# Industry's products as one stream of steps: two tiles ahead of layer 1's loop, 14 steps in each iteration

## Chip, cores and metric

The kernel runs on one core of one Trainium2 chip. The metric is the device time of one execution in microseconds. TensorE is called PE, VectorE DVE, ScalarE ACT, GpSimd POOL, and SyncE, which issues most transfers, SP.

## The reference

Four graph layers follow one another, each with a residual and a layer norm: `x = layernorm(x + layer(x))`. There are B = 8 batches, N = 2048 nodes and 64 features; `adj` is 2048 x 2048 and sparse. The change lies in layer 1, of which this matters:

```
h = x @ W
... agg, beta: attention of 64 hyperedges over the nodes
all_he = elu(beta * h + (1 - beta) * agg)
g = sum over a node's hyperedges e of coefs1[e] * all_he[e]
industry = (adj / deg) @ (x @ W_ind)
pair = stack([industry, g])
coefs2 = softmax(tanh(pair @ fcW + fcb) @ av)
out = sum over the pair of coefs2 * pair
```

So for each node there are two vectors, `industry` and `g`, and a two-way softmax mixes them.

## The kernel before

The nodes are split into NT = 16 tiles of 128. A row of a tile holds all 8 batches x 64 features, 512 numbers. The matrix of zeros and ones behind `adj` (the mask) is written to DRAM once in layer 0, one 1 MB block for each tile, and later layers load it again (`mask_tile`, and `mask_parts` for a block in four pieces).

A product of the mask with a 512-wide operand is split into a high and a low part of the operand, so one tile of Industry is 16 steps (`mt` = 0 to 15, one for each tile of the summed index) of two 128x512 matmuls, in `times_mask` (L1418). They add up in one PSUM buffer called `acc`, which comes from a pool with a single buffer. After the 16th step ACT reads it, multiplies it by the node's scale and writes it to SBUF as `ind` (L766), and DVE reads it again for the difference `dlt = industry - g` (L770).

Layer 1's main loop has NT + 3 iterations and is a software pipeline. At iteration t, different tiles are at different stages:

- `units` (marks u, v and s, for tiles t+1, t+2 and t): the hyperedge part, which ends in g. `sx`, `ST`, `gates`, `tau` and `ch0` prepare a tile; `gp0 z0 exp0 e0 w0` and `gp1 z1 exp1 e1 w1` are its two halves, each a chain PE, DVE, ACT, DVE, POOL; the two halves of all tiles share one PSUM buffer `gp`, so the next `gp` waits for the `e` before it. `dp` and `t3` belong to the fourth membership, and `ga`, `red` and `g` add up.
- `industry` (marks p and q): the 16 steps in pairs, and then `ind` and `dlt`.
- `mix_and_norm` (marks m, o and f, for tiles t-1, t-2 and t-3): `tr0 sT0 fc0 th0` for g, `tr1 sT1 fc1 th1` for industry, then `sub df sw`, and then the mix, the sum with the residual and the layer norm (`mult r s centre sq var rstd x2`).

The order within an iteration is written out by hand in the string `turns`, one word for each stage, and `program_order` fixes it on PE, DVE, ACT and POOL. SP's order is not fixed by it. A mark `p.i` is one pair of steps, four matmuls. In `turns` of the kernel before there are eight of them, and the last two stand at the end of the iteration.

Tile 0's product is done before the loop. `industry_early` makes a function `go_on(n)` that issues n more steps of it, and calls of it stand in the gaps of the end of layer 0 (5 and 3 steps) and of the start of layer 1 (4, 1, 2 and the rest, which is one), where the hyperedge attention is worked out in a chain of short instructions (`trhe`, `fche`, `sep`, `dnp`). Between them and the loop stand the stages of tile 0's unit and the first ones of tile 1's, and there are no steps of Industry there, nor in iteration t=0.

Tiles of SBUF that live for a short time are placed by hand in 16 homes (`b0_0` to `b0_15`), listed for each kind in `homes`.

Of the kernel before, what the change touches and what calls it, by code (L numbers as in the profile page):

```python
# [8 lines left out]
F32 = mybir.dt.float32  # L9

F32R = mybir.dt.float32r
AF = mybir.ActivationFunctionType
# [45 lines left out]
def r_(ap):  # L58
    return ap.bitcast(F32R)
# [3 lines left out]
def kernel(  # L63
# [450 lines left out]
    def layer1(  # L514
# [21 lines left out]
        with tc.tile_pool(name="fa", bufs=2) as fa:  # L536
# [10 lines left out]
            with program_order():  # L547
# [10 lines left out]
                    nc.vector.tensor_tensor(r_(dst[low]), full[low], dst[low], ALU.subtract)  # L558

                nc.vector.scalar_tensor_tensor(he, he, 1.0, agg, op0=ALU.min, op1=ALU.max)  # L560
                early[0](4)
                tr = ps_tr.tile([P, NP, P], F32, tag="tr", name="trhe")
                for pr in range(NP):
                    transpose(tr[:, pr, :], he[:, pr * P:(pr + 1) * P])
                heT = fa.tile([P, NP * P], F32, tag="hs", name="heT", bufs=3)
                nc.scalar.copy(heT, tr.rearrange("p r c -> p (r c)"))
                parts(agg1, agg)
                early[0](1)
                fc = ps_mm.tile([P, 2, QW], F32, tag="mm", name="fche")
                for h in range(2):  # L570
                    rs = slice(h * 64, (h + 1) * 64)
# [4 lines left out]
                    b_view(he), b_view(agg), -1.0,  # L576
                    vecs[:, 2, :].unsqueeze(1).to_broadcast([P, B, C]), op0=ALU.add, op1=ALU.mult,
                )
                early[0](2)
                sp = ps_tr.tile([P, QW], F32, tag="sm", name="sep")  # L580
                for b in range(B):
                    nc.tensor.matmul(
# [11 lines left out]
                nc.vector.tensor_copy(sums[:, 1, :], ese)  # L594
                parts(ext, sums)

                early[0](NT)
                dn = ps_tr.tile([P, NT, 2, B], F32, tag="tr", name="dnp")
                for j in range(NT):
                    nc.tensor.matmul(  # L600
# [15 lines left out]
        fw = stack.enter_context(tc.tile_pool(name="fw", bufs=2))  # L616
        mjp = stack.enter_context(tc.tile_pool(name="mj1", bufs=2))
        turn = {}
        homes = {"g": (0, 1, 2, 3), "dlt": (4, 5, 7), "ind": (14,), "r": (8, 9, 10),
                 "xr": (6, 12), "sq": (13,)}  # L620

        def row(tag, name):
            turn[tag] = turn.get(tag, -1) + 1
            home = homes[tag][turn[tag] % len(homes[tag])]
            return own.tile([P, BC], F32, tag=f"b0_{home}", name=name)
# [123 lines left out]
            dst[j] = g  # L749
            yield "g"  # L750

        def industry(j):

            if j:
                a = mask_tile(mjp, j, "l1")
                acc = ps_acc.tile([P, BC], F32, tag="acc", name=f"ind_{j}")
            else:
                acc = early[1]
            for mt in range(NT):
                if j:  # L760
                    times_mask(acc, a, i_hi, i_lo, mt)
                if mt % 2 == 1:
                    yield "i"
            sdeg = cols_of["sdeg"][:, j:j + 1]
            ind = row("ind", f"ind_{j}")
            nc.scalar.activation(ind, acc, AF.Copy, scale=sdeg)  # L766
            ind_of[j] = ind
            yield "ind"
            dlt = row("dlt", f"dlt_{j}")
            nc.vector.scalar_tensor_tensor(  # L770
                dlt, acc, sdeg, g_of[j], op0=ALU.mult, op1=ALU.subtract
            )
            dlt_of[j] = dlt
            yield "dlt"

        def mix_and_norm(j):

            ind, g, dlt = ind_of[j], g_of[j], dlt_of[j]
            xr = row("xr", f"xr_{j}")
            nc.sync.dma_start(xr, kept[j])
            r = row("r", f"r1_{j}")
# [75 lines left out]
        def layer2(j):  # L860
# [24 lines left out]

        g_of, ind_of, dlt_of = {}, {}, {}
        unit = {j: units(j, g_of) for j in range(NT)}
        mixer = {j: mix_and_norm(j) for j in range(NT)}  # L890
        product = {j: industry(j) for j in range(NT)}
        first = "sx ST gates tau ch0"
        second = "gp0 z0 exp0 ch1 dp t3 e0 w0 gp1 z1 exp1 e1 w1"
        turns = (
            "q.ind u.gp0 u.z0 q.dlt m.xg m.tr0 v.sx m.sT0 v.ST u.exp0 u.ch1 m.fc0 m.tr1 u.dp "
            "o.mult m.sT1 p.i m.th0 f.rstd u.t3 u.e0 p.i o.r m.fc1 v.gates u.w0 o.s u.gp1 p.i "
            "v.tau p.i m.th1 u.z1 s.ga p.i v.ch0 u.exp1 m.sub u.e1 o.centre s.red u.w1 f.x2 p.i "
            "m.df s.g o.sq m.sw o.var p.i p.i"
        )

        done = set()
# [18 lines left out]
        last = layer2_steps()  # L920
        with program_order():
            run(unit, 0, first)
            run(unit, 0, second)
            run(unit, 1, first)
            for t in range(NT + 3):
                now = {"p": (product, t), "q": (product, t - 1), "u": (unit, t + 1), "v": (unit, t + 2),
                       "s": (unit, t), "m": (mixer, t - 1), "o": (mixer, t - 2),
                       "f": (mixer, t - 3)}
                for turn_ in turns.split():
                    who, what = turn_.split(".")  # L930
                    run(*now[who], what)
                    if t > NT and 0 <= now[who][1] < NT:
                        next(last, None)
            a_first = mask_parts(own, 0, (11, 15, 0, 1), "l2")
            for _ in last:
                pass
            for j in range(NT):
                nc.gpsimd.tensor_tensor(
                    b_view(x2[:, j, :]), b_view(x2[:, j, :]),
                    bias2_sb.unsqueeze(1).to_broadcast([P, B, C]), ALU.add,  # L940
                )
# [12 lines left out]
    def layer0(  # L954
# [3 lines left out]

        h_sb, wb, wa, vecs, av_sb, pm, es, hgr, aggp, rden, early = layer1s
        raws, msk, terms, resid, norm, srow = {}, {}, {}, {}, {}, {}
        x1s, xTs, hps, hss, mds = {}, {}, {}, {}, {}

# [275 lines left out]
                    denp[0], mds[j], es[:, j, :], start=j == 0, stop=j == NT - 1  # L1240
                )

        def industry_early():


            a = mask_parts(own, 0, (4, 6, 13, 14), "l1")
            acc = ps_acc.tile([P, BC], F32, tag="acc", name="ind_0")

            def steps():
                for mt in range(NT):  # L1250
                    for part in (y_hi, y_lo):
                        nc.tensor.matmul(
                            acc, r_(a[:, mt, :]), r_(part[:, mt, :]),
                            start=mt == 0 and part is y_hi, stop=mt == NT - 1 and part is y_lo,
                        )
                    yield

            going = steps()

            def go_on(n):  # L1260
                for _ in range(n):
                    next(going, None)

            return go_on, go_on, acc

        mhalf = tile("mhalf", "mhalf0", (P, B), 1)
        nc.vector.memset(mhalf, -0.5)
        denp = []
# [17 lines left out]
        with program_order():  # L1286
# [6 lines left out]
            for j in range(NT + 1):  # L1293
# [4 lines left out]
                for g in range(8):  # L1298
# [9 lines left out]
                    elif g == 1:  # L1308
                        when(j - 1, normed, 1)
                        if j == NT:  # L1310
                            denp.append(
                                ps_p.tile([P, 2, 2, 4 * C], F32, tag="pp", name="denp")[:, 0, 0, 0:B]
                            )
                            denominators(0, NT - 1)
                            early.extend(industry_early())
                            early.pop(0)(5)
                        if first:
                            degrees(0)
                        when(j + 1, scaled, 0)
                    elif g == 2:  # L1320
                        when(j - 1, normed, 2)
                        when(j + 1, first_terms)
                    elif g == 3:
                        when(j - 2, project)
                        if j + 1 < NT:
                            for _ in product(j + 1):
                                pass
                        when(j - 1, to_features)
                        when(j + 1, compare, 0)
                        when(j + 1, scaled, 1)  # L1330
                        if j == NT - 2:
                            for t in range(len(kept_i)):
                                for y, kept_part in zip((y_hi, y_lo), kept_i[t]):
                                    nc.sync.dma_start(y[:, t, :], kept_part)
                        when(j + 2, mask, 0)
                        when(j + 2, mask, 1)
                    elif g == 5:
                        when(j + 1, compare, 1)
                        if j:
                            next(flags, None)  # L1340
                    elif g == 6:
                        when(j + 1, second_term)
                        when(j - 1, scores)
                        if j < NT:
                            when(j - 2, gather)
                        else:
                            project(NT - 1, h_first=True)
                            denominators(NT - 1, NT)
                            gather(NT - 2)
                            nc.vector.tensor_scalar(rden, denp[0], TINY, None, op0=ALU.max)  # L1350
                            nc.vector.reciprocal(rden, rden)
                    elif g == 7:
                        when(j + 1, degrees)
            early[0](3)
            gather(NT - 1)


    def short_program(top):
# [57 lines left out]
        def times_mask(acc, a, hi, lo, mt):  # L1416
            for part in (hi, lo):
# [2 lines left out]
                    start=mt == 0 and part is hi, stop=mt == NT - 1 and part is lo,  # L1420
                )

        def ln_tiles(pool):
            return lambda shape, tag, name: pool.tile(shape, F32, tag=tag, name=name)

# [4 lines left out]
        with tc.tile_pool(name="l0", bufs=1) as l0, tc.tile_pool(  # L1430
# [15 lines left out]
            with tc.tile_pool(name="l0s", bufs=2) as l0s, tc.tile_pool(  # L1446
# [2 lines left out]
            ) as ps_p:  # L1449
                layer0(  # L1450
                    own, l0s, rawp, mskp, ps_acc, ps_tr, ps_p, w_sb, emb_sb, bias_sb, bad, deg,
                    y_hi, y_lo, (h_sb, wb, wa, vecs, av_sb, pm, es, hgr, aggp, rden, early),
                )
                s1, dinv = cols_of["s1"], cols_of["dinv"]
                nc.vector.tensor_tensor(deg, deg, s1, ALU.mult)
# [694 lines left out]
```

## Time and profile before

| what | value |
|---|---|
| median of 3 runs | 1318.43 us (1313.73 to 1319.35) |
| the profiled execution, its own time | 1318.67 us |
| its span, first to last instruction | 1316.8 us |
| instructions | 19976 |
| granted PE clock, mean of the span | 0.973 |
| layer 1's loop, t=1 to t=15 (first gp to the last ind) | 760.7 to 1004.5 us |
| one steady iteration | 16.15 us |

The page gives, for each engine, the time it was busy. The chain of waits follows the work that ended last back from the last instruction, and its shares say which engine the end was waiting for. A table by stretch of time gives each engine's busy time and number of instructions in it, then the clock that PE was granted (1.00 is full speed), the share of the DMA engines that was busy, and GB/s. In a timeline, a bracket at the end of a line gives the time that the engine was idle before the instruction, and what ended it.

### The profile page before, as it was taken

What the parts mean: (1) busy time and instruction counts of PE and PEld (TensorE: products, weight loads), DVE (VectorE), ACT (ScalarE), POOL (GpSimd) and SP (SyncE); (2) the same over time, 40 slices, a digit from 0 to 9 for tenths busy, and PEclk for the clock granted to TensorE, in tenths of its full rate; (3) what the DMA queues carried; (4) which work ended last, traced back from release to release, by engine and by line L of the source; (5) the groups of instructions that cost most, each with busy time, mean ns of one, the idle gap of its engine ahead of it and who ended that gap; (6) DMA issues with size and microseconds to landing.
All of it is one profiled execution on the core that took longest, in us unless ns stands there. A gap on an engine that the chain in (4) does not pass through costs nothing.

```text
span 1316.8 us, 19976 instructions
## 1 busy us (share of the span) xinstructions
PE 1259.5 (96%) x7708; PEld 1002.4 (76%) x7708; DVE 885.0 (67%) x1595; ACT 368.4 (28%) x837; POOL 483.5 (37%) x403
## 2 busy tenths in 40 slices
PE   7999799999999999999999699999998899999996
PEld 6777588888888888888887467777776788888885
DVE  5555268888777877888664568878874655565544
ACT  3000001221122222221222356666664621111111
POOL 1000264444444444444411468888873600000000
PEclk9999799999999999999998589999998999999998
DMA  9887733332333332222272212222220133234551
GB/s 294 238 222 136 215 100 101 107 98 100 107 107 107 106 102 94 94 94 102 81 240 67 103 71 98 96 96 97 81 96 0 50 144 115 109 128 147 176 185 70
DMA packets 100791, 157.22 MB, mean 119 GB/s; under 512 B 12880, under 2 KB 64464, under 8 KB 94672
## 3 DMA queue, kind: packets, MB, share of 16 engines
q1 hardware_dynamic: 98208, 151.65, 35.7%
q10 hardware_dynamic: 2304, 4.20, 0.8%
q8 instruction: 63, 1.03, 0.3%
q0 software_dynamic: 176, 0.02, 0.1%
q14 instruction: 40, 0.33, 0.1%
HBM read 118.08 MB, written 37.76 MB: 118 GB/s over the span
## 4 chain that ended last, share of the span: by engine, by line
PE 89%; DVE 3%; DMA 2%; issue 2%; ACT 2%; POOL 1%; SPq 0%; ACTq 0%; DVEq 0%; POOLq 0%
PE pp L1104 25%; PE a L1418 18%; PE y2p L1067 9%; PE ind L1418 9%; PE y1p L490 8%; PE fc L805 3%; PE df L814 2%; PE gp L705 1%; PE yp L1508 1%; PE try L165 1%; PE trm L165 1%; PE aggp L1224 1%; PE hp L1192 1%; PE sgp L1171 1%; PE red L746 1%
## 5 line engine op out<-in xcount | busy, mean ns | idle before, releaser
L1115 DVE SCALAR_TENSOR_TENSOR r<-pp,emb_sb,r 128x256 f32<-128x256 f32 x512 | 247.4, 483 | 114.8 <-PE pp L1104 100.6
L1104 PE MATMUL pp<-w_sb,xT 64*128 64x256 f32 x1024 | 160.4, 390 | 1.7 <-DVE r L1115 1.7
L1104 PE MATMUL pp<-w_sb,y1T 64*128 64x256 f32 x1024 | 153.5, 376 | 0.0
L1104 PE MATMUL pp<-w_sb,y2T 64*128 64x256 f32 x1024 | 153.5, 376 | 0.0
L1053 POOL TENSOR_TENSOR r<-xs,bn 128x256 f32<-128x256 f32 x32 | 22.7, 731 | 277.2 <-issue 245.4
L1104 PEld LDWEIGHTS pp<-w_sb,xT 64*128 64x128 f32 x1024 | 94.4, 186 | 25.1 <-issue 14.9
L490 PE MATMUL y1p<-x_hi,m 128*128 128x512 f32 x256 | 106.2, 415 | 6.9 <-ACT x_hi L436 6.9
L1104 PEld LDWEIGHTS pp<-w_sb,y1T 64*128 64x128 f32 x1024 | 99.7, 187 | 10.9
L1104 PEld LDWEIGHTS pp<-w_sb,y2T 64*128 64x128 f32 x1024 | 99.6, 187 | 11.0
L1067 PE MATMUL y2p<-y_hi,msk 128*128 128x512 f32 x256 | 103.5, 404 | 0.0
L490 PE MATMUL y1p<-x_lo,m 128*128 128x512 f32 x256 | 103.0, 402 | 0.0
L1418 PE MATMUL ind<-y_hi,mj_l 128*128 128x512 f32 x240 | 101.7, 424 | 0.0
L1067 PE MATMUL y2p<-y_lo,msk 128*128 128x512 f32 x256 | 101.5, 397 | 0.0
L1418 PE MATMUL a<-v_hi,mj_l 128*128 128x512 f32 x256 | 100.1, 392 | 0.0
L1418 PE MATMUL a<-v_lo,mj_l 128*128 128x512 f32 x256 | 99.9, 391 | 0.0
L1418 PE MATMUL a<-y_lo,mj_l 128*128 128x512 f32 x240 | 95.1, 396 | 0.0
L1418 PE MATMUL a<-y_hi,mj_l 128*128 128x512 f32 x240 | 94.9, 396 | 0.0
L1418 PE MATMUL ind<-y_lo,mj_l 128*128 128x512 f32 x240 | 94.6, 394 | 0.0
L1009 POOL TENSOR_TENSOR ms<-msk,srow 128x1024 f32<-128x1024 f32 x32 | 89.8, 2807 | 5.3 <-DVE ms L1022 5.3
L737 POOL TENSOR_TENSOR ez<-ez,coef 128x1024 f32<-128x1024 f32 x32 | 69.8, 2182 | 56.3 <-DVE ez L735 54.3
L1001 DVE TENSOR_SCALAR msk<-adj 128x1024 fp32r<-128x1024 f32 x32 | 63.7, 2024 | 9.2 <-DMA adj<-in_at 9.2
L490 PEld LDWEIGHTS y1p<-x_hi,m 128*128 128x128 f32 x256 | 49.6, 194 | 19.0 <-ACT x_hi L436 6.9
(279 smaller groups left out, 2391.8 us busy)
## 6 DMA issues: line engine op xcount, KB each, us to landing
mj_l<-mask SPq DMA_DIRECT2D x46, 1024.0 KB, 4.9
raw<-in_at SPq DMA_DIRECT2D x32, 512.0 KB, 5.1
adj<-in_at SPq DMA_DIRECT2D x64, 256.0 KB, 3.8
mask<-msk SPq DMA_DIRECT2D x32, 512.0 KB, 4.6
xraw<-in_xn SPq DMA_DIRECT2D x8, 512.0 KB, 4.6
oh<-oh SPq DMA_DIRECT2D x32, 128.0 KB, 2.8
xT<-in_xt SPq DMA_DIRECT2D x16, 256.0 KB, 3.0
xs<-in_xn SPq DMA_DIRECT2D x16, 256.0 KB, 2.9
```

What stands on the lines that cost most here:

```text
L165: nc.tensor.matmul(dst, src, ident, start=True, stop=True, is_transpose=True)
L490: nc.tensor.matmul(accs[q][jj], r_(m[:, t, jj * P:(jj + 1) * P]), r_(part[:, mt, :]), start=i + h + t == 0 and part is x_hi, stop=i == 3 a ...
L737: nc.gpsimd.tensor_tensor(by_b(ez), by_b(ez), per_b(coef, 2 * i, 2), ALU.mult)
L805: nc.tensor.matmul(fc[:, h, :], fcw_sb[rs], sT[rs], start=True, stop=True)
L814: nc.tensor.matmul(df[:, b:b + 1], th[:, b % 2, (b // 2) * P:(b // 2 + 1) * P], av_sb, start=True, stop=True,)
L1001: nc.vector.tensor_scalar(r_(m), raws[j][h], 0.0, None, op0=ALU.is_gt)
L1009: nc.gpsimd.tensor_tensor(ms, m, srow[j].unsqueeze(1).to_broadcast([P, 8, P]), ALU.mult)
L1053: nc.gpsimd.tensor_tensor(r[:, 4 * bq * C:4 * (bq + 1) * C] .rearrange("p (h l c) -> p h l c", h=2, l=2), swapped(terms[j]["xs"], bq), bn. ...
L1067: nc.tensor.matmul(acc, r_(msk[j, mt // 8][:, mt % 8, :]), r_(part[:, mt, :]), start=mt == 0 and part is y_hi, stop=mt == NT - 1 and part ...
L1104: nc.tensor.matmul(pp[:, h, pl, :], terms[j][name][rs, 2 * bq + pl], w_sb[rs, k, dq * 4 * C:(dq + 1) * 4 * C], start=k == 0, stop=k == K - 1,)
L1115: nc.vector.scalar_tensor_tensor(rb, ppv[:, :, dd, :], emb_sb[:, j, d:d + 1], rb, op0=ALU.mult, op1=ALU.add)
L1418: nc.tensor.matmul(acc, r_(a[:, mt, :]), r_(part[:, mt, :]), start=mt == 0 and part is hi, stop=mt == NT - 1 and part is lo,)
```

## The change

The products of all tiles become one stream of 256 steps, held by an object `products` of a new class `industry`; `go_on(n)` issues the next n steps, whatever tile they belong to. When a tile's 16th step is issued, ACT's read of the accumulator is issued right behind it, and the result `ind` is kept in SBUF, in one of three homes (14, 11 and 15 in turn), until the mixing takes it. The masks of tiles 0 and 1 are loaded in four pieces each.

Ahead of the loop the stream now goes on by 5, 3, 4, 1, 2 and 3 steps where it did before (3 in place of the one that was left), then by 8 between tile 0's `t3` and `e0`, and by 6 after tile 1's `sx` to `ch0`, which now stand ahead of tile 0's `z1`. That is 32 steps, two tiles. In the loop each iteration has seven `p.i`, 14 steps, so that t=0 to t=15 issue the other 224. `dlt` moves to the mixing and is computed from `ind` in SBUF. The order in `turns` is new as a whole.

```diff
-        homes = {"g": (0, 1, 2, 3), "dlt": (4, 5, 7), "ind": (14,), "r": (8, 9, 10),
+        homes = {"g": (0, 1, 2, 3), "dlt": (4, 5, 7), "r": (8, 9, 10),
...
-                early[0](NT)
+                products.go_on(3)
                 dn = ps_tr.tile([P, NT, 2, B], F32, tag="tr", name="dnp")
...
-            sdeg = cols_of["sdeg"][:, j:j + 1]
-            ind = row("ind", f"ind_{j}")
-            nc.scalar.activation(ind, acc, AF.Copy, scale=sdeg)
-            ind_of[j] = ind
-            yield "ind"
-            dlt = row("dlt", f"dlt_{j}")
-            nc.vector.scalar_tensor_tensor(
-                dlt, acc, sdeg, g_of[j], op0=ALU.mult, op1=ALU.subtract
-            )
...
+        products.mask_of = lambda j: mask_tile(mjp, j, "l1")
+        ind_of = products.sums
+
+        def mix_and_norm(j):
+            ind, g, dlt = ind_of[j], g_of[j], row("dlt", f"dlt_{j}")
+            nc.vector.scalar_tensor_tensor(dlt, ind, 1.0, g, op0=ALU.mult, op1=ALU.subtract)
             yield "dlt"
...
         turns = (
-            "q.ind u.gp0 u.z0 q.dlt m.xg m.tr0 v.sx m.sT0 v.ST u.exp0 u.ch1 m.fc0 m.tr1 u.dp "
-            "o.mult m.sT1 p.i m.th0 f.rstd u.t3 u.e0 p.i o.r m.fc1 v.gates u.w0 o.s u.gp1 p.i "
-            "v.tau p.i m.th1 u.z1 s.ga p.i v.ch0 u.exp1 m.sub u.e1 o.centre s.red u.w1 f.x2 p.i "
-            "m.df s.g o.sq m.sw o.var p.i p.i"
+            "u.gp0 p.i m.dlt m.xg p.i f.rstd m.tr0 v.sx s.ga m.sT0 u.z0 u.exp0 m.fc0 o.mult m.tr1 "
+            "v.ST v.gates m.sT1 u.ch1 p.i o.r m.th0 u.dp u.t3 u.e0 u.w0 s.red o.s u.gp1 m.fc1 "
+            "m.th1 p.i s.g u.z1 p.i p.i v.tau m.sub u.exp1 p.i o.centre o.sq u.e1 v.ch0 m.df f.x2 "
+            "m.sw u.w1 o.var"
         )
...
             run(unit, 0, first)
-            run(unit, 0, second)
+            run(unit, 0, "gp0 z0 exp0 ch1 dp t3")
+            products.go_on(8)
+            run(unit, 0, "e0 w0 gp1")
             run(unit, 1, first)
+            products.go_on(6)
+            run(unit, 0, "z1 exp1 e1 w1")
...
                     who, what = turn_.split(".")
+                    if who == "p":
+                        products.go_on(2)
+                        continue
...
+        class industry:
+            def __init__(self, own, ps_acc, hi, lo):
+                early_masks = [
+                    mask_parts(own, 0, (4, 6, 13, 14), "l1"), mask_parts(own, 1, (7, 8, 11, 12), "l1b")
+                ]
+                self.mask_of, self.sums = early_masks.__getitem__, {}
+                self.steps = self.rows(own, ps_acc, hi, lo)
+
+            def rows(self, own, ps_acc, hi, lo):
+                for j in range(NT):
+                    a = self.mask_of(j)
+                    acc = ps_acc.tile([P, BC], F32, tag="acc", name=f"ind_{j}")
+                    for mt in range(NT):
+                        times_mask(acc, a, hi, lo, mt)
+                        if mt == NT - 1:
+                            ind = own.tile(
+                                [P, BC], F32, tag=f"b0_{(14, 11, 15)[j % 3]}", name=f"ind_{j}"
+                            )
+                            nc.scalar.activation(
+                                ind, acc, AF.Copy, scale=cols_of["sdeg"][:, j:j + 1]
+                            )
+                            self.sums[j] = ind
+                        yield
+
+            def go_on(self, n):
+                for _ in range(n):
+                    next(self.steps, None)
```

## The prediction

> **What bounds the kernel now.** I read the page's busy shares first, then the chain of waits in order of time, then busy time by stretch, then the timeline at a tile's end.
>
> ```profile
> PE 1259.5 (96%) x7708; PEld 1002.4 (76%) x7708; DVE 885.0 (67%) x1595; ACT 368.4 (28%) x837; POOL 483.5 (37%) x403
> PE 89%; DVE 3%; DMA 2%; issue 2%; ACT 2%; POOL 1%; SPq 0%; ACTq 0%; DVEq 0%; POOLq 0%
> ```
>
> PE holds 89% of the chain, so what counts is PE's instructions and PE's waits. The chain inside one turn of layer 1's loop:
>
> ```profile
> 784.62 1.86 PE ind L1418 x8
> 786.48 1.06 PE fc L805 x4
> ...
> 788.19 2.75 PE ind L1418 x12
> 790.94 0.86 PE red L746 x2
> 791.80 0.93 PE ind L1418 x4
> ...
> 794.42 1.97 PE ind L1418 x8
> ```
>
> These 32 matmuls of Industry take 1.86 + 2.75 + 0.93 + 1.97 = 7.51 us, **0.235 us each**. The same place recurs every 16.15 us (788.19, 804.35, 820.50). By stretch (PE, PEld, DVE, ACT, POOL busy; granted clock; DMA):
>
> ```profile
> 733.20:741.30 8.10, 3.77 (x8) 2.04 (x9) 4.43 (x9) 3.34 (x13) 2.94 (x3) 0.71 0.68 259
> 747.20:754.70 7.50, 4.71 (x12) 2.83 (x12) 4.33 (x10) 3.33 (x13) 4.72 (x3) 0.50 0.00 0
> 754.70:760.70 6.00, 2.90 (x4) 1.19 (x5) 3.83 (x9) 2.58 (x7) 5.89 (x4) 0.50 0.12 44
> 764.10:780.00 15.90, 15.90 (x68) 10.84 (x68) 7.81 (x14) 7.47 (x18) 10.57 (x9) 0.90 0.10 35
> 796.39:812.54 16.15, 16.15 (x81) 11.60 (x81) 12.88 (x20) 11.13 (x29) 13.04 (x10) 1.00 0.27 98
> ```
>
> The last row is a steady iteration: PE is never idle, DVE has 3.3 us free, POOL 3.1, ACT 5. The first three are the lead-in: PE idles half the time (gaps of 4.34, 3.32, 2.79 and 3.07 us, each waiting for DVE's ez) and is granted half clock. There a 128x512 matmul takes a slot of 0.427 us (ind at 706.07, then 706.50), not 0.235. A tile's end:
>
> ```profile
> 795.99 0.40 PE L1418 MATMUL ind<-y_lo,mj_l 128*128 128x512 f32 x1
> 796.22 0.63 PE L705 MATMUL gp<-agg,oh 128*128 128x512 f32 x2
> 796.43 0.69 ACT L766 ACTIVATE ind<-ind,sdeg 128x512 f32<-128x512 f32 x1 [1.79 <-PE ind L1418]
> ```
>
> The tile's last matmul ends at 796.39 and ACT reads the accumulator until 797.12. Meanwhile PE goes on with gp, because the next tile's first matmul comes only at 800.61: today the read is covered.
>
> **What the skill says.** The Trainium skill, "TensorE: Matmul & The Clock Gate", Part 1, says that PE falls to half rate after an idle window of about 3.4 us and returns after a busy one, the windows running freely. The trace agrees: 0.427 against 0.235 us, and clock 0.50 over the gaps. The same page, "Architectural detail", says that matmuls stay in order and ACT and DVE are strict FIFO, so a wait holds up all behind it; the trace shows each engine in its written order. "PSUM — Partial Sum Buffer", the summary of rules, says to read one bank while the matmul runs in another. Industry has one accumulator (a pool of one buffer), and the kernel before shows only the covered case.
>
> **The change, part by part**, against the profiled run's own 1318.67 us (span 1316.8; the median of the runs is 1318.43, so the two may be used alike).
>
> *A. Fewer matmuls per iteration.* 28 in place of 32: 4 x 0.235 = 0.94 us less. I walked the new turns with the durations above. From gp0 at 0, PE does gp0, 8 ind (to 2.35), tr0, sx, fc0, tr1 (5.18), 4 ind, dp, red, gp1 (8.72), fc1 (9.78), 16 ind (13.54), df (15.22). What it waits for arrives in time: e0 on DVE ends near 6.4 (gp1 wants it at 8.07), sub near 12.3 (df at 13.54), e1 near 14.1 (the next gp0 at 15.22). POOL's 13.3 us fit. So 15.2 per iteration: for t = 2 to 15, 14 x 0.94 = **-13.1**.
>
> *B. Tile ends inside the iteration.* Two tiles are done ahead and a tile needs eight "p.i", an iteration has seven. So tile 2 ends at the first p.i of t=1, tile 3 at the second of t=2, on to the seventh of t=7; t=8 has none; then first to seventh again for t=9 to 15. On PE the new list puts nothing between p.i 1 and 2, nor between 4, 5, 6 and 7 (m.dlt, m.xg, s.g, u.z1, v.tau, m.sub, u.exp1 belong to other engines). An end at 1, 4, 5 or 6 thus exposes ACT's read, with all of PE's queue behind the next tile's first matmul. Price: 0.17 (the last matmul lasts 0.40, its slot is 0.23) + 0.04 + 0.69 + about 0.07 to start, + 0.09 because the first matmul after a break takes a slot of 0.32 (778.12 to 778.44): **1.05 us**, more than the iteration's gain. In t>=2 they are t = 4, 5, 6, 9, 12, 13, 14: 7 x 1.05 = 7.4. Bounds: 0 if something I overlooked covers them (a wait added to a queue without idle time gains nothing), 1.3 if ACT is behind with th1; I take 1.05. Besides, an end at 6 puts the read ahead of tau and exp1 on ACT, so e1 ends about 0.35 after PE wants it (twice), and an end at 2 makes sT0, and fc0 behind it, 0.25 late (twice): 1.2. Together **+8.6**.
>
> *C. The lead-in*, from sep (PE free at 726.71) to the start of t=2 (gp0 at 780.23).
> - go_on(3) ahead of dnp: before, one step stood there (1.06 us). Now that step ends tile 0, ACT reads it (+0.9), and four matmuls of tile 1 follow (4 x 0.427 = 1.7): dnp, and with it rec, hgr, sx, gp0, starts about 2.5 late (1.85 at full clock).
> - go_on(8): 16 matmuls after dp, which now ends near 739.4. Half clock at first, then full: about 4.5 us, of which 4.34 was idle. gp1 comes at about 744.3 instead of 741.33.
> - unit 1's sx and go_on(6): 12 matmuls, then ACT's read of tile 1 ahead of exp1 in ACT's queue, and unit 1's gates ahead of z1 on DVE. gp1 to the next gp0: 0.65 + 0.73 + 2.82 + 0.2 + 0.69 + 1.1 + 1.25 + 0.14 = 7.6 against 5.9. So t=0 starts near 751.9 (before 747.23).
> - t=0: 28 more matmuls, 6.6 us at full clock, against 2.79 + 3.07 idle; starting at half clock, the iteration takes about 13 (13.5 before, at half clock throughout). t=1 starts near 764.5 to 765.5 (before 760.70).
> - t=1 took 19.5 before, part at half clock. Warm it takes 15.2 + 1.05 (an end at p.i 1) = 16.2.
> So t=2 starts at about 781.7 instead of 780.23: **+1.5**. Bounds -2 (windows fall well) and +5 (little of it warm).
>
> *D. The rest.* dlt on DVE from SBUF: 0.68 (the row of L822) for 0.745, in DVE's slack. ind tiles in homes 14, 11, 15: next written after their readers are long done. Tile 1's four mask loads (home 7 free at 700.4, when the last pp ends) are on SP ahead of S and oh, 1.3 us of issue, in place of two early pieces of layer 2's first mask; those two now load after t=15, with some 40 us before they are wanted. xr_1 waits in home 12 until go_on(6) is over, 30 us before its use. Layer 1's own mask loads keep one iteration of lead for 5 us of landing. All zero, covered by PE's queue; if SP came late, tile 2's load would be the first to show, by up to 5 us once. At t=16 the read of the last tile no longer stands ahead of sT0: about **-0.2**.
>
> Sum: -13.1 + 8.6 + 1.5 - 0.2 = -3.2, so 1318.67 - 3.2 = **1315.5 us**.
>
> **Rivals.**
> 1. *Ends covered.* If ACT's read costs PE next to nothing and the lead-in gains from a warm clock: -13.1 + 1 - 1 = -13, near 1306; with half of B and C as forecast, -13.1 + 4.3 + 1.5 - 0.2 = -7.5, 1311. For it: ACT is 5 us idle per iteration. Against it: one accumulator, adjacent p.i.
> 2. *Half clock in the lead-in (slower).* The 60 new or moved matmuls from go_on(3) to the end of t=0 at 0.427 are 25.6 us against 13.5 us of idle time: 12.1 late, +1.6 for two exposed reads; t=1, warm, gives back 3.3: C becomes +10.4 and the sum +5.7, **1324.4**. It decides from C = 4.9 on, where gain and loss cancel. For it: 0.50 there now. Against it: denser work is what raises the clock (704.6 to 709 did).
> 3. *A new bound.* Should e1 come late in every iteration (it has 1.1 us of slack), each 0.3 us over that costs 4 in all: 1320 for 0.3, 1325 for 0.7.
>
> **Numbers.** The forecast has 0.56, rival 1 0.26 (its half-price case included), rivals 2 and 3 0.18. A measurement of this kernel tells about 0.5%, 6.6 us, from no change. Of the forecast's and rival 1's mass about 0.29 lies below 1311.8; above 1325.0 lie parts of rivals 2 and 3, 0.14. The range, 1307 to 1324, takes in the bounds of B and C.
>
> **What would show it.** A: ind matmuls per iteration 28, and 15.2 us between like places in t = 3, 7, 8, 10, 11. B: t = 4, 5, 6, 9, 12, 13, 14 longer by about 1 us, with PE waiting for ACT's ind. C: dnp 2 to 2.5 us later; clock above 0.5 from about 740; t=2 within 3 us of 781.7. Periods of 15.2 throughout would break B, 16 or more throughout would break A, and a start of t=2 after 787 would break C.

## The result and the profile after

The changed kernel takes **1331.34 us** (median of 7 runs, 1327.42 to 1338.67) beside 1319.35 us for the kernel before on the same chip (7 runs, 1313.73 to 1321.51): ratio 1.0114, 95% interval 1.0091 to 1.0138 (the two medians alone stand at 1.0091, its lower end). It is about 1% slower; the forecast was 1315.5, with 1324 as the upper end. The profiled execution of the changed kernel is the slowest of its seven (1338.67, span 1336.9), so stages are compared below and the whole is not taken from it.

Busy shares and the chain's shares by engine, from the page of the changed kernel:

```profile
PE 1266.5 (95%) x7708; PEld 1002.3 (75%) x7708; DVE 919.2 (69%) x1595; ACT 365.6 (27%) x837; POOL 485.0 (36%) x403
...
PE 74%; DVE 13%; issue 5%; ACT 4%; DMA 2%; POOL 0%; SPq 0%; DVEq 0%; ACTq 0%; POOLq 0%
```

PE's share of the chain fell from 89% to 74% and DVE's rose from 3% to 13%. DVE has as many instructions as before (1595), but is busy 34 us longer. So some of them must last longer, and that is the first thing to look for. By stretch (length, then PE, PEld, DVE, ACT, POOL busy; granted clock; DMA), each from one gp0 to the next (t=2, 3, 4):

```profile
784.40:799.72 15.32, 15.23 (x78) 10.87 (x78) 12.97 (x19) 9.13 (x21) 10.04 (x8) 1.00 0.29 104
799.72:816.45 16.73, 15.41 (x79) 10.77 (x78) 15.65 (x21) 9.64 (x24) 12.85 (x10) 1.00 0.28 95
816.45:834.21 17.76, 15.69 (x79) 10.69 (x78) 16.68 (x22) 11.27 (x32) 13.22 (x10) 1.00 0.26 89
```

The first iteration takes 15.3 us, close to the forecast 15.2. Then DVE's busy time goes from 13.0 (12.9 in the kernel before) to 15.7, the iteration to 16.7, and PE, which had no idle time before, has over a microsecond of it. Which instructions grew is read from the timeline of DVE, POOL and PE in the iteration of t=3 (start, duration, engine, line, operation, output and inputs, shapes):

```profile
799.72 1.91 POOL L738 TENSOR_TENSOR ez<-ez,coef 128x1024 f32<-128x1024 f32 x1 [1.83 <-DVE ez L736]
799.72 0.70 PE L706 MATMUL gp<-agg,oh 128*128 128x512 f32 x2
...
800.09 2.08 DVE L762 SCALAR_TENSOR_TENSOR dlt<-ind,g 128x512 f32<-128x512 f32 x1
...
801.58 1.72 POOL L767 TENSOR_TENSOR r<-g,xr 128x512 f32<-128x512 f32 x1
...
804.56 0.69 DVE L804 SCALAR_TENSOR_TENSOR dlt<-sw,dlt 128x512 f32<-128x512 f32 x1
...
806.47 1.05 POOL L693 TENSOR_TENSOR d<-h,sig 128x512 f32<-128x512 f32 x1
...
806.75 1.31 DVE L808 SCALAR_TENSOR_TENSOR r<-dlt,r 128x512 f32<-128x512 f32 x1
...
807.99 1.21 DVE L736 SCALAR_TENSOR_TENSOR ez<-gp,d 128x1024 f32<-128x1024 f32 x1
...
809.25 0.72 PE L706 MATMUL gp<-agg,oh 128*128 128x512 f32 x2 [1.32 <-DVE ez L736]
...
812.71 1.91 POOL L693 TENSOR_TENSOR d<-h,sig 128x1024 f32<-128x1024 f32 x1
...
813.41 1.76 DVE L813 SCALAR_TENSOR_TENSOR r<-s,r 128x512 f32<-128x512 f32 x1
```

Four DVE instructions have the same shape and two inputs in SBUF: dlt (L762), mult (L804), the addition r (L808) and centre (L813). Alone, one lasts 0.68 us. dlt starts 0.37 us after POOL's ez and ends 0.54 us after ez's end: it stood still until POOL was all but done, 2.08 us in all. r waits for POOL's d in the same way (1.31), and centre for the next d (1.76). They too end 0.54 and 0.55 us after POOL's instruction, and so does every long one in this loop (0.54 to 0.56), wherever it started. mult, in between, meets only POOL's rstd and lasts 0.69. No semaphore shows any of this: the timeline prints no wait beside these lines, the instruction is just long.

What PE feels of it is a wait of 1.32 us for e0 ("ez" on DVE) ahead of gp1. PE's waits in the loop of the changed kernel, from gp0 of t=2 to tr0 of t=16 (line waited for: us in total, times, longest):

```profile
PE gp L706 <- DVE ez L736: 11.5, 11, 1.3
PE ind L1383 <- ACT ind L1409: 5.4, 7, 0.8
PE fc L787 <- ACT sT L779: 1.4, 2, 0.7
```

and in the same stretch of the kernel before:

```profile
PE fc L805 <- ACT sT L797: 1.5, 2, 0.8
```

So there are **two new waits**: eleven for e0, and seven at exposed tile ends. The second is the one the forecast counted, at the seven iterations it named. One end in the timeline of PE:

```profile
828.49 0.39 PE L1383 MATMUL ind<-y_lo,mj_l 128*128 128x512 f32 x1
829.65 0.50 PE L1383 MATMUL ind<-y_hi,mj_l 128*128 128x512 f32 x1 [0.78 <-ACT ind L1409]
```

1.16 us from start to start where 0.23 is the rule: 0.93 us.

The two waits don't simply add up. Beside the 16.7 us of an iteration without an end, one with an end at p.i 4, 5 and 6 takes 17.8, 17.4 and 17.1, and the one with an end at p.i 1 (t=9) again 16.74: there the wait for e0 that follows is 0.25 us in place of 1.3.

The stages of the profiled executions are the lead-in, the loop and the way out of it (from tr0 of t=16 to layer 2's first matmul). They are counted from trhe (just ahead of the lead-in), since what comes earlier differs by up to 7 us between executions (trhe at 716.0 to 723.4 in the kernels below) without a change to account for it:

| kernel (profiled execution) | trhe to gp0 of t=2 | t=2 to tr0 of t=16 | to layer 2's first matmul | sum |
|---|---|---|---|---|
| before | 59.1 | 224.2 | 44.1 | 327.4 |
| after | 61.5 | 234.1 | 48.2 | 343.7 |

The loop lost 10 us where 4.5 were to be gained, the way out of the loop lost 4.1, the lead-in 2.3. (In the kernel before, gp0 of t=2 starts at 780.07; the forecast reads 780.23.)

### The profile page after: what moved, and what is told of

Its sections match the earlier page's. It is cut to its first block, busy times and chain, and to the rows that moved or that the text cites. A ratio compares the mean times of both kernels' runs of the same rounds, so it can differ in the third digit from the quotient of the medians.

```text
span 1336.9 us, 19950 instructions
## 1 busy us (share of the span) xinstructions
PE 1266.5 (95%) x7708; PEld 1002.3 (75%) x7708; DVE 919.2 (69%) x1595; ACT 365.6 (27%) x837; POOL 485.0 (36%) x403
## 4 chain that ended last, share of the span: by engine, by line
PE 74%; DVE 13%; issue 5%; ACT 4%; DMA 2%; POOL 0%; SPq 0%; DVEq 0%; ACTq 0%; POOLq 0%
PE pp L1091 25%; PE a L1383 18%; PE y2p L1054 9%; PE y1p L490 6%; PE ind L1383 4%; DVE d L716 2%; DVE dlt L762 2%; DVE ez L736 2%; DVE gp L713 1%; ACT gp L718 1%; PE try L165 1%; PE yp L1505 1%; DVE r L813 1%; PE aggp L1211 1%; PE hp L1179 1%
## 5 line engine op out<-in xcount | busy, mean ns | idle before, releaser
L1383 PE MATMUL ind<-y_hi,mj_l 128*128 128x512 f32 x224 | 93.9, 419 | 6.2 <-ACT ind L1409 6.2
L1383 PE MATMUL ind<-y_lo,mj_l 128*128 128x512 f32 x224 | 90.0, 402 | 0.0
L738 POOL TENSOR_TENSOR ez<-ez,coef 128x1024 f32<-128x1024 f32 x32 | 61.6, 1925 | 59.2 <-DVE ez L736 59.2
L1383 PEld LDWEIGHTS ind<-y_hi,mj_l 128*128 128x128 f32 x224 | 43.4, 194 | 29.1 <-issue 11.4
```

Of the source, the lines that this page charges most:

```text
L738: nc.gpsimd.tensor_tensor(by_b(ez), by_b(ez), per_b(coef, 2 * i, 2), ALU.mult)
L1383: nc.tensor.matmul(acc, r_(a[:, mt, :]), r_(part[:, mt, :]), start=mt == 0 and part is hi, stop=mt == NT - 1 and part is lo,)
```

## The experiments

**Theory 1.** A DVE instruction with two SBUF inputs stands still while POOL runs an instruction that reads SBUF tiles; the new order puts dlt, r and centre into such stretches, e0 comes late and PE waits. The Trainium skill has this on the page "SBUF — State Buffer", section "Who interferes with whom": "A DVE instruction with two SBUF inputs contends with a GpSimd instruction that reads SBUF"; its "Summary: rules for kernel authors" says that the second one to issue blocks until the first finishes. The traces agree: the three long instructions above start after POOL's and end 0.54 to 0.55 us after its end, where 0.68 us is their whole length alone. **Theory 2.** PE's new order and its exposed tile ends make the loss, and the long DVE instructions only fill time in which DVE would be idle.

### One input of dlt from PSUM (dlt_psum)

```
-            nc.vector.scalar_tensor_tensor(dlt, ind, 1.0, g, ...)
+            other = fc_of[j - 1][:, 0, :] if j else g     # a PSUM tile
+            nc.vector.scalar_tensor_tensor(dlt, ind, 1.0, other, ...)
```

> The changed kernel, except that the second operand of dlt is not g in SBUF but the fc tile of the tile before, in PSUM, so that dlt has one SBUF input (this leaves the subtraction of g out of the mix). Order and every other instruction are unchanged. Theory 1 (dlt takes 2.08 us because a DVE instruction with two SBUF inputs waits until POOL's running ez has finished): dlt falls to about 0.75 us at the same place, e0 and gp1 come about 1.3 us earlier, and the iterations fall from 16.7 to 15.3-15.6 us: 14 x 1.2, so about 1315 to 1319 us. Theory 2 (the new order's own chain of waits on PE, ACT and DVE sets 16.7 us, and dlt only fills idle time): iterations stay at 16.5 or more, 1328 to 1333 us.

Measured: 1325.03 us (19 runs), ratio to before 1.0045 (1.0027 to 1.0063). The groups of DVE in the loop (busy us and mean ns at the end):

```profile
L810 DVE SCALAR_TENSOR_TENSOR r<-dlt,r 128x512 f32<-128x512 f32 x13 | 19.1, 1465 | 0.1
L815 DVE SCALAR_TENSOR_TENSOR r<-s,r 128x512 f32<-128x512 f32 x12 | 18.1, 1506 | 0.0
...
L763 DVE SCALAR_TENSOR_TENSOR dlt<-ind,fc 128x512 f32<-128x512 f32 x12 | 8.1, 673 | 0.0
```

In the same place, again 0.37 us after the start of POOL's ez, dlt falls from 2083 to 673 ns because one input lies in PSUM. That is the mechanism by itself. PE's wait for e0 falls from 11.5 to 2.5 us. The time fell between the two expectations: iterations without an end take 15.8 us, and r and centre still wait (1465 and 1506 ns).

### dlt in another place (dlt_moved), and all three (lock_free)

```
 dlt_moved:  u.gp0 p.i [m.dlt] m.xg ... m.fc0  ->  u.gp0 p.i m.xg ... m.fc0 d.dlt o.mult
 lock_free:  besides: o.mult o.r m.tr1 (was: o.mult m.tr1 v.ST v.gates m.sT1 u.ch1 p.i o.r)
                      v.tau o.centre m.sub (was: v.tau m.sub u.exp1 p.i o.centre)
```

> The changed kernel with dlt's instruction as it is (two SBUF inputs), but moved in DVE's order from ahead of z0 to just ahead of mult, where POOL runs rstd, which reads only 8 numbers a partition. Theory 1: dlt takes 0.68 us there, z0 starts 1.3 us earlier, iterations 15.3 to 15.7 us, total 1315 to 1320 us; centre (1.76 us) and r (1.31 us) stay long, since they still run against POOL's ch0 and ch1. Theory 2: dlt may get shorter, the iterations stay at 16.5 or more.

> The changed kernel with every PE instruction in its place; only VectorE's three instructions with two SBUF inputs are moved to where GpSimd reads no tile: dlt and the addition r directly ahead of and behind mult (GpSimd is then on rstd), centre ahead of sub. Theory 1 (VectorE waits for GpSimd's SBUF reads, three times per iteration, and the late e0 and e1 hold PE): all of 0.69 us, VectorE's busy time per iteration back from 15.7 to 13 us, iterations 15.3 to 15.6 where no tile's end is exposed, and 1313 to 1320 us, since the exposed ends and the lead-in stay. Theory 2 (PE's new order itself, with the matmuls bunched behind gp1, or the tile ends, make the loss): 1324 us or more, as with dlt alone moved.

Measured: dlt_moved 1324.24 us (18 runs), ratio 1.0049 (1.0031 to 1.0068), 4 us above its expected range although its wait for e0 falls to 0.9 us and its loop to 224.2; lock_free 1321.21 us (14 runs), ratio 1.0019 (1.0003 to 1.0035). PE's waits and one iteration without a tile's end in lock_free:

```profile
PE ind L1391 <- ACT ind L1417: 5.4, 7, 0.8
PE gp L706 <- DVE ez L736: 1.4, 2, 0.7
```

```profile
799.66:814.95 15.29, 15.29 (x77) 10.78 (x76) 13.73 (x21) 10.95 (x29) 13.35 (x9) 1.00 0.31 104
```

The wait for e0 is nearly gone, the tile ends are untouched, and the iteration is back near the forecast's 15.2. In ratios, 0.95 of the 1.14% loss is taken back by moving three DVE instructions, with PE's order unchanged: theory 1 holds for the larger part, and theory 2 alone is out. What r and centre cost beyond dlt is not settled: the two loops differ by 0.3 us, and the intervals of the two ratios overlap by a little. lock_free ended 1 us above its expected range. r is still 1464 ns on average (ga follows rstd on POOL and catches it), and one iteration, from tr0 to tr0, took 19.0 us: behind an exposed end at p.i 6 the clock was 0.57 for 6.5 us.

### The same wait put into the kernel before (before_sbuf, before_lock2)

```
 before_sbuf:   dlt, acc, sdeg, g_of[j]  ->  dlt, ind, 1.0, g_of[j]       (place unchanged)
 before_lock2:  besides: u.z0 [q.dlt] m.xg ... o.r  ->  u.z0 m.xg ... o.r q.dlt m.fc1
```

> The kernel before with one edit: dlt takes ind from SBUF instead of the accumulator in PSUM, at its old place, where POOL has mostly finished its reading. Theory 1: dlt takes about 0.68 us, nothing else changes, the time stays within 0.3% of the kernel before. If two SBUF inputs were slow by themselves, or if the difference from SBUF were the whole loss: dlt above 1.3 us in most iterations, and 1322 us or more.

> The kernel before with dlt from the SBUF copy of ind (which alone changed nothing), and dlt moved behind the addition r, where GpSimd is reading ez. Theory 1 (the wait belongs to the pair of engines, not to the change): dlt 1.9 to 2.1 us in place of 0.69, VectorE's busy time per iteration 12.9 to about 14.2; it had 3.3 us free, so 0 to 8 us slower, 1318 to 1326. Theory 2 (dlt is slow in the changed kernel for another reason of its new surroundings): 0.69 and no change.

Measured: before_sbuf 1317.40 us (14 runs), ratio 0.9990 (0.9968 to 1.0012); before_lock2 **1330.61 us** (6 runs), ratio 1.0095 (1.0066 to 1.0124). The timeline of before_lock2, and PE's waits in its loop:

```profile
823.07 0.68 DVE L827 SCALAR_TENSOR_TENSOR r<-dlt,r 128x512 f32<-128x512 f32 x1
...
823.30 2.22 POOL L737 TENSOR_TENSOR ez<-ez,coef 128x1024 f32<-128x1024 f32 x1 [1.59 <-DVE ez L735]
...
823.67 2.39 DVE L770 SCALAR_TENSOR_TENSOR dlt<-ind,g 128x512 f32<-128x512 f32 x1
```

```profile
PE df L814 <- DVE th L810: 4.5, 12, 0.4
PE fc L805 <- ACT sT L797: 1.5, 2, 0.8
```

With dlt at its old place, its input's home makes no difference. One turn further on it lasts 2.39 us, and the kernel before becomes as slow as the changed one, without any of the change. This exceeded the expected 0 to 8 us. DVE is busy 14.5 us of an iteration of 16.8 and still has 2.2 us free, but not where it is needed: gates, z1 and sub stand behind dlt, and df on PE waits for sub twelve times. An iteration with nothing else takes 16.75 in place of 16.15 us, which is 7 of the loop's 12 us; most of the rest is clock: in three iterations the granted clock fell to about 0.5 behind df, and they took 18.0 to 18.3 us. The fence also shows the reverse: r started first, so POOL's ez needed 2.22 us where 1.91 is its length alone.

### The stream with the old turn order (old_order)

```
 turns: the old list, with q.ind and the last p.i left out and q.dlt named m.dlt
```

> The changed kernel (stream of steps, two tiles ahead, 14 steps per iteration, dlt from SBUF) with the order of the turns of the kernel before, less its last p.i and with dlt where it was. There mult, r and centre take 0.68 us in the kernel before, because POOL waits for DVE then. Theory 1: DVE has no instruction longer than its row in the kernel before, iterations without an exposed read take 15.2 us, those with one (six, at the first, third and fourth p.i) about 16.2, total 1310 to 1316 us. Theory 2 (any order with 14 steps is bound by another chain): 16 us or more throughout, 1320 us or more.

Measured: **1311.22 us** (22 runs), ratio 0.9953 (0.9937 to 0.9969), as expected, and faster than the kernel before. Its four DVE instructions take 0.68 to 0.77 us on average. Two iterations, without and with an exposed end, and PE's waits in the loop:

```profile
838.05:853.26 15.21, 15.21 (x77) 10.85 (x76) 13.41 (x21) 10.82 (x29) 14.28 (x11) 1.00 0.22 59
883.69:899.95 16.26, 15.48 (x78) 10.78 (x77) 12.88 (x20) 11.12 (x29) 13.02 (x10) 1.00 0.31 97
```

```profile
PE ind L1383 <- ACT ind L1409: 3.9, 5, 0.8
PE fc L787 <- ACT sT L779: 1.4, 2, 0.7
```

15.21 without and 16.26 with an exposed end: **1.05 us for an end**, the forecast's price, and 0.94 less per iteration, again its number. The loop takes 217.2 us in place of 224.2. What the change does with its stream is worth some 6 us; what its new turn order does costs some 21 us (1.61% between the two ratios).

### What a tile's end costs (short_read, dp_between, gp1_between)

```
 short_read (on lock_free):  activation(ind[:, 0:C], acc[:, 0:C], ...); dlt and tr1 take g for ind
 dp_between (on dnp_early):  m.tr1 u.dp o.mult m.sT1 p.i m.th0  ->  m.tr1 p.i u.dp o.mult m.sT1 m.th0
 gp1_between (on dp_between): o.s u.gp1 p.i v.tau p.i  ->  o.s p.i u.gp1 v.tau p.i
```

> lock_free with ScalarE's read of Industry's accumulator cut from 512 to 64 columns; Industry's products are still multiplied but left out of the mix, which takes g in their place. Theory (the prediction's part B: an exposed end costs PE the length of this read, and ends at p.i 5 and 6 delay e1 besides): a read of 0.2 us in place of 0.69; iterations with an end at p.i 1 and 4 16.2 down to 15.7 us, at 5 and 6 17.2 and 19.0 down to 15.8; 14 iterations 223.8 down to 217 to 219; 1314 to 1317 us. Rival (the long iterations at p.i 5 and 6 come from VectorE or from the clock, not from the read): within 1.5 us of lock_free's 1321.2.

> As the run before it, and dp put between the two adjacent steps p.i 1 and p.i 2, so that a tile's end at p.i 1 (t = 2 and 9, and t = 1) has 1.05 us of PE work behind it. Theory (an exposed end costs PE 0.93 us): three ends fewer, 2.5 us less than the run before. Rival (PE waits later for e1 in any case, and the end is hidden in that): no change, or slower where t3 comes late behind dp.

> dp_between (1311.5 us) with p.i 3 ahead of gp1, so that ends at p.i 2 and 3 have fc1 and gp1 behind them and only an end at p.i 4 is exposed. Theory (0.93 us for each exposed end, and e1 has over 2 us of slack here): two ends fewer, about 2 us less, 1309.5. Rival (gp1 0.93 us later makes sub and df late): 1311.5 to 1316.

short_read, which leaves Industry's products out of the mix: 1309.64 us (17 runs), ratio 0.9954 (0.9932 to 0.9975), 0.65% below lock_free and some 4 us below its expected range. PE's waits in its loop:

```profile
PE ind L1391 <- ACT ind L1417: 2.8, 7, 0.4
PE gp L706 <- DVE ez L736: 1.4, 2, 0.7
```

The wait at an end halves (0.78 to 0.40), as expected. That is 2.6 us; the loop became 5.5 us shorter (223.8 to 218.3, as expected), and most of the rest is the iteration of 19.0 us, which took 16.0 at full clock. Iterations with an end at p.i 5 stayed at 16.9 (17.2 in lock_free): an end delays PE, DVE's mult slides into POOL's ga and lasts 1.76 us, r behind it slides into d (1.42), and gp1 waits 0.70. A tile's end thus costs more in this order than its own wait, because it also brings back the other one.

dp_between 1311.47 us (6 runs), ratio 0.9936 (0.9914 to 0.9958), and its base dnp_early 0.9951: 2 us in the expected direction, and within the interval. gp1_between 1313.39 us (22 runs), 0.9978 (0.9962 to 0.9993): the two intervals do not meet, so it is slower than dp_between, as its rival had it; its trace shows eight waits at ends in the loop (4.8 us) where dp_between has four (3.1 us). Neither is a step beyond old_order that the runs could show.

### The lead-in (dnp_early)

```
-                products.go_on(3)      # ahead of dnp
+                products.go_on(1)
-            products.go_on(8)          # behind t3
+            products.go_on(10)
```

> The stream with the old turn order (1311.2 us), and go_on(3) ahead of dnp cut to go_on(1), go_on(8) made go_on(10), so that tile 0's read is not waited for ahead of dnp. Theory (the prediction's part C: go_on(3) ahead of dnp delays everything behind it): dnp 2 to 2.5 us after its place behind trhe comes forward, two more matmul pairs fit in the gap behind dp that waits for e0 anyway; 1309 to 1310 us. Rival (gp1 of unit 0 becomes late by the four matmuls added there, so it is the same sum): 1311.

This kernel is old_order with the two edits. Measured: 1311.92 us (6 runs), ratio 0.9951 (0.9931 to 0.9970), the same as old_order: the time that its rival named. In the trace dnp follows trhe after 6.7 us in place of 8.3, and t=2 starts 55.8 us after trhe in place of 58.6; the timed runs don't show these 2.9 us. Their gain stays open.

### The way out of the loop (x2_early, old_way_out)

From tr0 of t=16 to layer 2 the changed kernel needs 48.2 us in place of 44.1. ACT and PE there, in the timelines of the changed kernel:

```profile
1017.01 0.69 ACT L1409 ACTIVATE ind<-ind,sdeg 128x512 f32<-128x512 f32 x1 [2.67 <-PE ind L1383]
1017.60 0.62 ACT L818 ACTIVATE sq<-r 128x512 f32<-128x512 f32 x1
1018.12 2.00 ACT L829 ACTIVATE x<-r,rstd 128x64 f32<-128x64 f32 x8
...
1020.09 0.57 ACT L779 COPY sT<-trm 128x512 f32<-128x512 f32 x1
```

```profile
1020.71 1.86 PE L787 MATMUL fc<-sT,fcw_sb 64*128 64x512 f32 x4 [1.55 <-ACT sT L779]
...
1025.30 2.08 PE L787 MATMUL fc<-sT,fcw_sb 64*128 64x512 f32 x4 [1.69 <-ACT th L782]
```

The last tile's read, which the order before had behind sw, now holds up sq and x2, and sT0 waits behind them. fc lasts 2.08 us in place of 1.13: half clock, from about 1021 to 1038. The kernel before falls to half clock here too, but later on its way out and for a shorter time, from about 1013 to 1020.

```
 x2_early (on lock_free):  m.th1 p.i ... m.df f.x2 m.sw  ->  m.th1 f.x2 p.i ... m.df m.sw
 old_way_out (on after):   turns if t < NT - 1 else the old list without its last p.i
```

> lock_free with ScalarE's x2 (2.0 us) issued behind th1 in place of behind sq. Theory (the loop's way out, 48.1 us from tr0 at t=16 to layer 2 in place of 44.1, is long because the last tile's read holds up sq and x2 on ScalarE, sT0 waits behind them and PE falls to half clock): 44 to 45 us there, 1317 to 1318 us if x2 fits in ScalarE's idle 1.8 us of the loop. Rival (the way out is long because PE's order there leaves it short of work): 48 us there, 1321 us or more.

> The changed kernel, with the old turn order (less its last p.i) from t=15 on; t=0 to 14 as changed. Theory (the way out of the loop is 4 us longer because of the order in which ACT and PE reach it, whatever the loop before it): 44 us from tr0 at t=16 to layer 2 in place of 48.1, and 3.5 to 4.5 us less than the changed kernel, 1327. Rival (the longer way out follows from the late state in which this loop leaves VectorE and GpSimd, or from a clock window that falls there by chance): 47 to 48 us there, 1330 to 1332.

x2_early: **1331.72 us** (6 runs), ratio 1.0116 (1.0090 to 1.0142), 1.0% slower than lock_free. The theory failed; the time lies in the rival's open range, but not for its reason. ACT's idle time was no room either: x2 stands ahead of the tile's read and of exp1, and PE's wait at an end grows:

```profile
PE ind L1391 <- ACT ind L1417: 11.1, 7, 2.6
PE gp L706 <- DVE ez L736: 3.1, 6, 0.6
```

The loop took 238.3 us in place of 223.8: 7.4 us are waits, and clock lost behind them is part of the rest (one iteration took 22.5 us at a mean clock of 0.77, four others ran at 0.90 to 0.91). On the way out sT0's wait did shrink (0.68 for 1.55), but the clock stayed at half and the stage took 47.0 us. old_way_out: 1329.90 us (6 runs), ratio 1.0096 (1.0072 to 1.0121); its way out took 45.4 us, and its last iteration of the loop fell to half clock instead. The two ratios, 1.0096 and 1.0114, differ by less than their intervals. So the 4 us go with a longer stretch of half clock, and probably come from it; what starts it there is **not settled**.

| kernel (profiled execution) | trhe to t=2 | t=2 to t=16 | to layer 2 | ratio of the runs to before |
|---|---|---|---|---|
| after | 61.5 | 234.1 | 48.2 | 1.0114 |
| dlt_psum | 61.5 | 227.4 | 48.2 | 1.0045 |
| dlt_moved | 58.3 | 224.2 | 47.6 | 1.0049 |
| lock_free | 59.4 | 223.8 | 48.1 | 1.0019 |
| short_read | 58.5 | 218.3 | 47.7 | 0.9954 |
| x2_early | 59.4 | 238.3 | 47.0 | 1.0116 |
| old_way_out | 61.5 | 235.5 | 45.4 | 1.0096 |
| old_order | 58.6 | 217.2 | 44.0 | 0.9953 |
| dnp_early | 55.8 | 217.2 | 43.9 | 0.9951 |
| before_lock2 | 59.1 | 236.1 | 45.4 | 1.0095 |

## Why the prediction was wrong

- **D's price of dlt failed, and A's walk with it.** D put dlt at "0.68 ... in DVE's slack", and A's walk used DVE's durations of before at new places on the time axis. dlt measured 2.08, r 1.31, centre 1.76. The walk had e0 end 6.4 us after gp0; in the trace it ends at 809.20, 9.5 after gp0 (799.72). Of the 3.1 us, 2.8 are dlt's 1.4, r's 0.6, and 0.8 that gates wait for ST, which ACT does behind a late exp0. gp1 wants e0 at 8.07, so PE waits 1.3. It is a missed wait between two engines, not a mis-sized term: the forecast has no term for it. The loop was to take 219.7 us and took 234.1; of these 14.4 us, 10.3 went when three DVE instructions moved (lock_free).
- **A's price held**: 0.94 per iteration, 15.2 to 15.3 without a wait (15.21 in old_order, 15.29 in lock_free, 15.32 in the changed kernel's first).
- **B held** in place and in price: seven ends at the iterations named, 0.93 by the timeline and 1.05 by the iterations of old_order, forecast 1.05. Its other term, 1.2 us for a late e1 and a late sT0, names other waits than came: ends at p.i 5 push DVE into POOL's reads, so that gp1 waits for e0 (0.71 us each time in lock_free).
- **C held**: +2.3 us in the profiled execution, forecast +1.5 and bounds -2 to +5. go_on(3) delayed dnp by 1.7, not 2.5; the forecast had 1.85 for full clock. That the sum came so near is partly luck: t=0 took 15.9 us at a mean clock of 0.71 in this execution, 13.1 at 0.87 in that of lock_free, and 13 was forecast. In the executions in which t=0 took some 13 us, and whose lead-in is that of the changed kernel, it is within 1 us of the kernel before (58.3 to 59.4 in the table).
- **D's way out failed**: -0.2 forecast, +4.1 measured, with a longer stretch of half clock behind a wait of sT0. The tile's read did leave its place ahead of sT0, but it landed ahead of sq and x2, and sT0 stands behind those.
- **The rivals.** Rival 3 ("a new bound") had the right kind of cause, a DVE result that is late in every iteration, but at the wrong place (it named e1 ahead of gp0, and it was e0 ahead of gp1), too small (1320 to 1325), and without its reason, the blocked DVE instructions. Rival 2 did not come true: the lead-in was near its forecast. (By its own terms gain and loss cancel at C = 4.7, not 4.9.)
- **What the profile of before showed and was not read.** One of its r instructions was long, beside a POOL instruction that reads SBUF:

```profile
992.16 1.28 POOL L743 TENSOR_TENSOR g<-g,ez 128x512 f32<-128x512 f32 x1
992.32 1.67 DVE L826 SCALAR_TENSOR_TENSOR r<-dlt,r 128x512 f32<-128x512 f32 x1
```

On DVE's side a group's mean of 757 ns, where its neighbours had 681, was the only sign of it in the list of groups. The old order kept the other twelve ahead of POOL: r starts some 0.2 us before POOL's ez, and ez is the one that waits. That shows on the two pages, before and after:

```profile
L737 POOL TENSOR_TENSOR ez<-ez,coef 128x1024 f32<-128x1024 f32 x32 | 69.8, 2182 | 56.3 <-DVE ez L735 54.3
```

```profile
L738 POOL TENSOR_TENSOR ez<-ez,coef 128x1024 f32<-128x1024 f32 x32 | 61.6, 1925 | 59.2 <-DVE ez L736 59.2
```

The block was there all along; the new order changed which engine pays for it, from POOL, which had time, to DVE, which PE waits for.

## What to carry to other kernels

Before moving a DVE instruction with two SBUF inputs, lay POOL's instructions beside its new place: its duration is a property of the place and not of the instruction, and no wait is printed for it. Look for it as one group of equal shapes with two durations. Idle time of an engine, summed over an iteration, is no room for a delay: before_lock2 left DVE 2.2 us free per iteration and lost 12 us; x2_early used ACT's idle time and lost 1.0%. And two waits in one iteration don't simply add up: a wait that comes early can shorten one that comes later, as at t=9.

## What the runs showed of the hardware that was not expected

- A blocked DVE instruction of 128x512 ended 0.54 to 0.56 us after the POOL instruction that held it, in every case in the changed kernel's loop (behind ez, d, ga and once xg). So its price was what was left of POOL's instruction plus 0.55 us, in place of 0.68.
- The block goes both ways, by who starts first: POOL's ez of 128x1024 lasts 1.90 us alone, 2.2 to 2.3 with a DVE instruction of 0.68 started ahead of it; xg lasts 1.29 alone and 1.72 behind dlt.
- Not every POOL instruction blocks for its whole length: rstd (128x8, 1.67 us, inputs in SBUF) was running for 0.96 us when mult started, and mult took 0.69 us. By the rule of the page "SBUF — State Buffer" (section "Who interferes with whom"), read literally, mult should have waited; the measurement decides. Where mult started just ahead (by up to 0.02 us in dlt_psum), it was rstd that lasted longer, 2.2 us. Both would fit a lock that rstd needs only at its start, for its few numbers; no run here tests that.
- A DVE instruction with one PSUM input did not wait: z1's first instruction (L713) started at 810.31, in the middle of POOL's ez (809.28 to 811.18), and took 0.69 us, where it took 0.70 in the kernel before.
- A short wait in a dense loop can be followed by several microseconds at half clock: 0.57 for 6.5 us in lock_free, behind a wait of 0.8 us at an end at p.i 6, and about 0.5 for some 3 us in three iterations of before_lock2, behind waits of 0.4 us. The Trainium skill, "TensorE: Matmul & The Clock Gate", Part 1, ties half rate to an idle window of about 3.4 us; here the visible waits were much shorter, with df's sixteen small matmuls behind them, and most such waits had no such effect. When it strikes is not settled by these runs.
